# Gated recurrent cell: half B's h and z moved from fp32 to three bf16 parts, r of half B into half A's bank

## Chip, core and metric

The kernel runs on one core of one Trainium2 chip. The metric is the device time of one launch in microseconds, as the median of the runs. Times without a unit in this text are microseconds.

## What is computed

A gated recurrent layer over 512 time steps, with 8 sequences and 512 units, and the input added to its output:

```python
def step(h, x_t):
    fused = sigmoid(concat([x_t, h]) @ w_W + w_b)
    r, z = split(fused, 2)                      # "hidden_state", "output_state"
    m = x_t @ wx_W + wx_b + r * (h @ wh_W + wh_b)
    return z * h + (1.0 - z) * tanh(m)
out = x + scan(step, cond_1024, x)
```

All arrays are float32. x is (8, 512, 512), the weights are w_W (1024, 1024), wx_W (512, 512), wh_W (512, 512). Three products need the state of the step before: those of r, of z and of h (`h @ wh_W`); the products with x_t don't, and are made ahead of time.

## The kernel before

**Layout.** The 512 units lie as 4 chunks k of the contraction (128 partitions each) and, on the output side, as 4 column groups j of TensorE: a matmul with 32 columns of weights (the "weights" here are the state, 4 steps x 8 sequences, of which only the running step's 8 are not zero) writes PSUM partitions 32j to 32j+32. The moving operand is the model's weights. The output's 128 units of a group are split into half A (64) and half B (64), so that one half can be updated while the other is multiplied. Half A is chunks 0 and 1 of the state, half B chunks 2 and 3.

**TensorE.** Three PSUM tiles per group of 4 steps (two sets, used in turn) take the recurrent products: A holds h, z, r of half A (192 columns), B holds r and h of half B (128), C holds z of half B (64). The order within a step is written out by hand: `ORDER = "A0 B0 A1 A2 A3 B1 B2 B3 C0 C1 C2 C3"`, letter for tile, digit for chunk; each entry is 4 fp32 matmuls, one per column group. An fp32 matmul stands in the trace as two records. After them come 7 matmuls of the x products for a later group (`take(later, 7)`; 192 columns, into `xp`); they run out 11 steps before the end, and steps 0 to 4 take 8 or fewer of 384 columns in their place. The accumulated x side is copied into A, B, C ahead of a group by ScalarE (`spread`), and turned by VectorE (`turn_x`) for the part of m that r doesn't multiply.

**Everything else of a step**, in program order: `turn_r`, `turn_h`, `turn_z` of half A (VectorE transposes 32x32 blocks from PSUM: `tr`, `md1A`, `tz`; ScalarE takes sigmoids), `memory(0, q)` (a VectorE scan over pairs makes m, ScalarE's tanh follows, one for each chunk q), the transposes of r and h of half B, `update(0, 0)` (a scan over triples makes the new state of chunk 0), the transpose of z of half B, `update(0, 1)`, then `memory` and `update` of half B. The engines run their queues in order. `idle` memsets on VectorE carry waits. ScalarE copies the new state into the next step's scan input, GpSimd adds x for the output (`ot`, line 507), and SyncE stores chunks of 16 steps and loads x.

**Names and lines.** `mm` is line 188 for all matmuls; `act` line 216; `scan` line 358 (tiles `m`, `hTA`, `hTB`); `turned` line 374; `turn_h` line 390; `spread` line 251; `turn_x` line 256; idle memsets lines 400 and 505; output add line 507. `hT` is the state, `md0` and `md1` the scan inputs of `memory`, `hd0` that of `update`. The A0 of a step needs `update(0, 0)` of the step before, A1 needs `update(0, 1)`, A2 and A3 those of half B.

Of the kernel before, what the change touches and what calls it, by code (L numbers as in the profile page):

```python
# [21 lines left out]
DVE_FILL = 23  # L22
IDLE = 3
# [14 lines left out]
XP = {"A": slice(0, 192), "X": slice(192, 320), "C": slice(320, 384), "B": slice(384, 512)}  # L38
# [3 lines left out]
def tile_cond_rnn_residual(  # L42
# [5 lines left out]
    wa_d: bass.AP,  # L48
    wb_d: bass.AP,
    wb3_d: bass.AP,  # L50
# [76 lines left out]
    wa = const.tile([P, NQ, NQ, 192], F32, name="wa")  # L127
    for k in range(NQ):
        nc.sync.dma_start(out=wa[:, k], in_=wa_d[k])
    wb = const.tile([P, NQ, NQ, 192], F32, name="wb")  # L130
    nc.sync.dma_start(out=wb[:, :3], in_=wb_d)
    nc.sync.dma_start(out=wb[:, 3], in_=wb3_d)

    def wh(bank, k, j):
        return wa[:, k, j] if bank == "A" else wb[:, k, j, {"C": slice(0, 64), "B": slice(64, 192)}[bank]]
# [3 lines left out]
    def pair(n, name, rows, slots):  # L139

        return const.tile([P, 2, rows, slots], F32, name=name).rearrange("p c n s -> p n c s")

    NH = 2 * GS
    hT = [[pair(n, f"hT{n}{i}", 32, 3) for i in range(NH)] for n in "AB"]

    md0 = [[pair(n, f"md0{n}{i}", 32, 2) for i in range(2)] for n in "AB"]
    md1 = [[pair(n, f"md1{n}{i}", 32, 2) for i in range(2)] for n in "AB"]
    hd0 = [[pair(n, f"hd0{n}{i}", B, 3) for i in range(2)] for n in "AB"]  # L150
# [7 lines left out]
    for j in range(NQ):  # L158
        nc.vector.memset(ones[32 * j : 32 * j + 1, j], 1.0)

    nc.scalar.activation(const.tile([P, 1], F32, name="table"), zeros[:, :1], AF.Sigmoid)
    for n, t_ in enumerate(hd0[0] + hd0[1] + md0[0] + md0[1] + hT[0] + hT[1]):
# [3 lines left out]
    idle = const.tile([P, IDLE], F32, name="idle")  # L166
# [8 lines left out]
    def state(hf, i, slot=2):  # L175

        s = i % GS
        return hT[hf][i % NH][:, B * s : B * s + B, :, slot]

    ctx.enter_context(tc.manual_schedule())  # L180
    banks = [
        {n: psum.tile([P, w], F32, name=f"{n}{q}") for n, w in BANKS.items()}
        for q in range(2)
    ]
# [8 lines left out]
    for t_ in list(banks[0].values()) + list(banks[1].values()):  # L193
        mm(t_, none, none[:, :1].broadcast_to([P, t_.shape[1]]), start=True)
# [8 lines left out]
    nc.vector.tensor_copy(bias, xps[0])  # L203
    for hf in range(2):
        for slot in (0, 2):
            nc.vector.tensor_copy(
                state(hf, 0, slot), hin[:, 2 * hf : 2 * hf + 2].rearrange("p c b -> p b c")
            )
# [35 lines left out]
    def part(g, c0, c1):  # L244

        return late(g)[:, c0 - 256 : c1 - 256] if c0 >= 256 else xps[g % 2][:, c0:c1]

    def spread(g, names):

        for n in names:  # L250
            nc.scalar.copy(banks[g % 2][n], part(g, XP[n].start, XP[n].stop))

    def turn_x(g, e):

        c0 = XP["X"].start + 32 * e
        nc.vector.transpose(md1[e // 2][g % 2][:, :, e % 2, 1], part(g, c0, c0 + 32))
# [67 lines left out]
    spread(0, "BCA")  # L324
    for e in range(NQ):
        turn_x(0, e)

    pool_done = {}
    for i in range(T):
        g, s = divmod(i, GS)  # L330
        c, t = divmod(i, TC)
        ps = banks[g % 2]
# [5 lines left out]
        for n in (ORDER if i else FIRST).split():  # L338
            if n == "x":
                take(first[1], 1)  # L340
                continue
            bank, k = n[0], int(n[1])
            hs = hT[k // 2][i % NH][:, :, k % 2, 2]
            for j in range(NQ):
                j = (j + turn[0]) % NQ
                to = ps[bank] if i or bank != "A" else xps[0][:, XP["A"]]
                mm(to[32 * j : 32 * j + 32, :], hs, wh(bank, k, j))
# [8 lines left out]
        def scan(c_, out_, d0, d1):  # L356

            return nc.vector.tensor_tensor_scan(  # L358
                *[t_[:, :, c_].rearrange("p n c s -> p (n c s)") for t_ in (out_, d0, d1)],
                0.0,  # L360
                ALU.mult,
                ALU.add,
            ).ins

        pa = ps["A"] if i else xps[0][:, XP["A"]]
        raw = {
            "h": (pa[:, :HU], ps["B"][:, HU:]),
            "z": (pa[:, HU : 2 * HU], ps["C"]),
            "r": (pa[:, 2 * HU :], ps["B"][:, :HU]),
        }  # L370

        def turned(n, hf):
            t_ = work.tile([P, 2, 32], F32, tag=f"t{n}{hf}", name=f"t{n}{hf}_{i}")
            inst = nc.vector.transpose(t_.rearrange("p c n -> p (c n)"), raw[n][hf]).ins  # L374
            return t_[:, :, rows], inst

        r_done = [None, None]
        h_done = [None, None]

        def turn_r(hf):  # L380
            tr, _ = turned("r", hf)
            r_done[hf] = act(
                ("r", hf, g % 2, s),
                md0[hf][g % 2][:, rows, :, 1].rearrange("p n c -> p c n"),
                tr,
                AF.Sigmoid,
            )

        def turn_h(hf):
            inst = nc.vector.transpose(  # L390
                md1[hf][g % 2][:, :, :, 0].rearrange("p n c -> p c n"), raw["h"][hf]
            ).ins
            h_done[hf] = inst
            if hf == 0 and i + 1 - NH in pool_done:
                tc.add_manual_dep(inst, pool_done[i + 1 - NH].name, SYNC)

        def turn_z(hf):
            tz, _ = turned("z", hf)
            if hf == 0:
                inst = nc.vector.memset(idle[:, IDLE - 1 :], 0.0).ins  # L400
                tc.add_manual_dep(inst, h_done[0].name, SYNC)
            act(
                ("zc", hf, i % 2),
                hd0[hf][i % 2][:, :, :, 2].rearrange("p n c -> p c n"),
                tz,
                AF.Sigmoid,
                scale=-1.0,
            )

        ms = [  # L410
            work.tile([P, 2, B, 2], F32, tag=f"m{hf}", name=f"m{hf}_{i}").rearrange("p c n s -> p n c s")
            for hf in range(2)
        ]

        def memory(hf, q):

            c_ = slice(q, q + 1)
            scan(c_, ms[hf], md0[hf][g % 2][:, rows], md1[hf][g % 2][:, rows])
            act(("n", hf, q, i % NH), state(hf, i, 1)[:, :, c_], ms[hf][:, :, c_, 1], AF.Tanh)

        def update(hf, q):
            s1 = (i + 1) % GS
            new = hT[hf][(i + 1) % NH][:, B * s1 : B * s1 + B]
            return scan(slice(q, q + 1), new, hd0[hf][i % 2], hT[hf][i % NH][:, rows])

        turn_r(0)
        turn_h(0)
        turn_z(0)
        memory(0, 0)
        memory(0, 1)  # L430
        turn_r(1)
        turn_h(1)
        update(0, 0)
        turn_z(1)
        tc.add_manual_dep(update(0, 1), r_done[1].name, SYNC)
# [3 lines left out]
        if i == T - 1:  # L439
            nc.gpsimd.tensor_tensor(  # L440
                ot[:, t, :2, :].rearrange("p c n -> p n c"),
                x_of(c, slice(0, 2), t, 1).rearrange("p c n -> p n c"),
                state(0, T),
                ALU.add,
            )
        memory(1, 0)
        memory(1, 1)
        update(1, 0)
        update(1, 1)
        for hf in range(2):  # L450
            act(("h", hf, (i + 1) % NH), state(hf, i + 1, 0), state(hf, i + 1), AF.Copy)
# [3 lines left out]
        o, u = divmod(i, 2 * GS)  # L455
        nxt, two = o + 1 < NG // 2, o + 2 < NG // 2
        if i == 0:
            nc.scalar.copy(odd[0], xps[1][:, 256:512])
            spread(1, "A")
            turn_x(1, 0)  # L460
        ahead = 2 * o + (1 if u < 3 else 2 if u < 7 else 3)
        if ahead < NG:
            turn_x(ahead, (u + 1) % GS)
        if u == 0:
            spread(2 * o + 1, "B")
            if o and nxt:
                nc.scalar.copy(reg(GA), reg(BE))
        elif u == 1:
            spread(2 * o + 1, "C")
# [3 lines left out]
        elif u == 2 and nxt:  # L473
            last = odd[(o + 1) % 2][:, :HALF]
            nc.vector.tensor_tensor(last, reg(GA), both, ALU.add)
        elif u == 3 and nxt:
            if o:
                nc.vector.tensor_tensor(even[:, :HALF], reg(BE), both, ALU.add)
            spread(2 * o + 2, "A")
        elif u == 4 and nxt:  # L480
            if o == 0:
                nc.scalar.copy(odd[1], xps[1][:, 256:512])
            spread(2 * o + 2, "B")
# [3 lines left out]
        elif u == 5 and nxt:  # L487
            spread(2 * o + 2, "C")
# [6 lines left out]
        elif u == 7 and nxt:  # L495
            spread(2 * o + 3, "A")
# [7 lines left out]
        for n in range(IDLE - 1):  # L504
            nc.vector.memset(idle[:, n : n + 1], 0.0)
# [100 lines left out]
```

## Time and profile before

| | |
|---|---|
| median of 3 runs (lowest, highest) | 1679.92 (1678.17, 1680.07) |
| span of the profiled execution | 1670.8 |
| median less that span | 9.1 |
| mean granted TensorE clock | 0.999 |
| TensorE, VectorE, ScalarE, GpSimd busy | 1659.0, 1090.5, 1029.9, 301.9 |
| matmul records | 56238 |

The span runs from the first to the last instruction of one profiled execution; the runs' times hold what lies around it too. An engine's busy time is that in which one of its instructions ran; matmuls overlap in TensorE and their ends are modelled, so its share says that it always had a matmul under way, not that it worked at its full pace. In the timeline a row is the start, the duration, the engine, the line, the operation, output and inputs by the tiles' names, the shape, and how many like it follow (xN); in brackets stands the idle time before it and what ended it. In the rows of groups the total busy time and the mean ns of one stand behind the bar, then the engine's idle time before them.

### The profile page before, as it was taken

Reading aid. Unit: us, or ns where it says so; the run is one execution under the profiler, and the core shown is the slowest. Engines: PE = TensorE matmul, PEld = TensorE weight load, DVE = VectorE, ACT = ScalarE, POOL = GpSimd, SP = SyncE. Lnnn points to the kernel's source line nnn. Section 1 sums busy time; section 2 is a strip of 40 time slices with the busy share of each in tenths; the row PEclk is TensorE's granted clock in tenths of the full one; section 3 lists DMA queues with packets and bytes.
Section 4 is the critical chain, followed back from the end, with each engine's and each line's share of the span. In section 5 each row is a group of like instructions: output and inputs, shape, how many; then the busy total and the mean of one; then the engine's idle time right before and its main releaser. Section 6 shows DMA issues by size and latency. Waiting matters only on the chain.

```text
span 1670.8 us, 129875 instructions
## 1 busy us (share of the span) xinstructions
PE 1659.0 (99%) x56238; PEld 1637.5 (98%) x56238; DVE 1090.5 (65%) x9387; ACT 1029.9 (62%) x5822; POOL 301.9 (18%) x1281
## 2 busy tenths in 40 slices
PE   8999999999999999999999999999999999999998
PEld 5999999999999999999999999999999999999997
DVE  6666666666666666666666666666666666666666
ACT  3666666666666666666666666666666666666665
POOL 1111111111111111111111111111111111111111
PEclk9999999999999999999999999999999999999999
DMA  4000000000000000000000000000000000000000
GB/s 179 17 5 17 18 18 17 17 6 17 17 18 18 5 17 18 17 17 5 18 17 17 18 11 12 18 17 17 18 5 17 17 18 17 5 17 12 11 12 10
DMA packets 11525, 31.40 MB, mean 19 GB/s; under 512 B 1220, under 2 KB 1732, under 8 KB 10824
## 3 DMA queue, kind: packets, MB, share of 16 engines
q1 hardware_dynamic: 10800, 22.94, 4.0%
q8 instruction: 440, 7.21, 1.8%
q14 instruction: 133, 1.09, 0.2%
q10 hardware_dynamic: 152, 0.16, 0.0%
HBM read 14.70 MB, written 8.39 MB: 14 GB/s over the span
## 4 chain that ended last, share of the span: by engine, by line
PE 98%; DVE 1%; DMA 0%; issue 0%; ACT 0%
PE A L188 44%; PE B L188 23%; PE xp L188 20%; PE C L188 12%; DMA rows<-in_bias_dram 0%; DVE tr L374 0%; DVE m L358 0%; DVE tz L374 0%; DVE md1B L390 0%; DVE md1A L390 0%; DVE hTA L358 0%; DVE bias L203 0%; ACT hTB L216 0%; ACT xp L224 0%; DVE rows L120 0%
## 5 line engine op out<-in xcount | busy, mean ns | idle before, releaser
L188 PE MATMUL A<-wa,hTA 128*32 128x192 f32 x8176 | 638.2, 329 | 2.3 <-DVE hTA L358 2.3
L188 PE MATMUL B<-wb,hTA 128*32 128x128 f32 x8192 | 573.8, 273 | 0.0
L188 PE MATMUL A<-wa,hTB 128*32 128x192 f32 x8176 | 507.4, 326 | 0.5 <-DVE hTB L358 0.5
L188 PEld LDWEIGHTS B<-wb,hTA 128*32 128x32 f32 x8192 | 471.2, 122 | 1.4 <-issue 0.2
L374 DVE STREAM_TRANSPOSE tr<-A 128x64 f32<-128x64 f32 x511 | 127.7, 250 | 463.5 <-PE A L188 463.5
L188 PE MATMUL B<-wb,hTB 128*32 128x128 f32 x8192 | 398.9, 273 | 0.0
L188 PEld LDWEIGHTS A<-wa,hTA 128*32 128x32 f32 x8176 | 385.4, 123 | 7.6 <-DVE hTA L358 4.0
L188 PEld LDWEIGHTS A<-wa,hTB 128*32 128x32 f32 x8176 | 372.9, 122 | 2.7 <-DVE hTB L358 0.8
L216 ACT ACTIVATE md0A<-tr 128x16 f32<-128x16 f32 x512 | 112.3, 219 | 421.0 <-DVE tr L374 421.0
L507 POOL TENSOR_TENSOR ot<-xin,hTB 128x16 f32<-128x16 f32 x503 | 125.9, 250 | 1324.5 <-DVE hTB L358 1314.0
L188 PEld LDWEIGHTS B<-wb,hTB 128*32 128x32 f32 x8192 | 321.5, 122 | 0.1
L188 PE MATMUL C<-wb,hTA 128*32 128x64 f32 x8192 | 289.4, 219 | 0.0
L188 PE MATMUL C<-wb,hTB 128*32 128x64 f32 x8192 | 288.9, 220 | 0.2 <-issue 0.2
L188 PEld LDWEIGHTS C<-wb,hTA 128*32 128x32 f32 x8192 | 266.7, 122 | 0.0
L188 PE MATMUL xp<-tw,sx 128*32 128x192 f32 x2976 | 237.2, 326 | 0.1
L188 PEld LDWEIGHTS C<-wb,hTB 128*32 128x32 f32 x8192 | 229.2, 123 | 0.4 <-issue 0.4
L358 DVE TENSOR_TENSOR_SCAN hTB<-hd0B,hTB 128x24 f32<-128x24 f32 x1024 | 157.8, 195 | 101.0 <-ACT hTB L216 99.8
L358 DVE TENSOR_TENSOR_SCAN hTA<-hd0A,hTA 128x24 f32<-128x24 f32 x1024 | 191.0, 187 | 0.0
L188 PE MATMUL xp<-wx,xin 128*32 128x192 f32 (+1 forms) x2048 | 182.4, 331 | 0.7 <-issue 0.5
L216 ACT ACTIVATE hd0B<-tz 128x16 f32<-128x16 f32 x512 | 115.2, 225 | 93.7 <-DVE tz L374 93.7
L216 ACT ACTIVATE hTB<-hTB 128x16 f32<-128x16 f32 x512 | 120.5, 235 | 79.8 <-DVE hTB L358 72.3
L216 ACT ACTIVATE hTB<-m 128x8 f32<-128x8 f32 x1024 | 160.6, 206 | 0.0
(92 smaller groups left out, 2489.6 us busy)
## 6 DMA issues: line engine op xcount, KB each, us to landing
xin<-in_x_dram SPq DMA_DIRECT2D x31, 256.0 KB, 3.5
out_dram<-ot SPq DMA_DIRECT2D x31, 256.0 KB, 2.2
wx<-in_wx_dram SPq DMA_DIRECT2D x4, 768.0 KB, 7.1
wa<-in_wa_dram SPq DMA_DIRECT2D x4, 384.0 KB, 8.9
wb<-in_wb_dram SPq DMA_DIRECT2D x1, 1152.0 KB
wb<-in_wb_dram SPq DMA_DIRECT2D x1, 384.0 KB, 11.1
out_dram<-ot SPq DMA_DIRECT2D x1, 192.0 KB, 3.9
head<-in_xh_dram ACTq DMA_DIRECT2D x1, 144.0 KB, 5.0
```

Of the source, the lines that this page charges most:

```text
L188: nc.tensor.matmul(out_, lhsT, rhs, start=start, stop=False, skip_group_check=True)
L216: inst = nc.scalar.activation(out_, in_, func, **kw).ins
L358: return nc.vector.tensor_tensor_scan(*[t_[:, :, c_].rearrange("p n c s -> p (n c s)") for t_ in (out_, d0, d1)], 0.0, ALU.mult, ALU.add,).ins
L374: inst = nc.vector.transpose(t_.rearrange("p c n -> p (c n)"), raw[n][hf]).ins
L507: return engine.tensor_tensor(ot[:, t, 2 * hf : 2 * hf + 2, :].rearrange("p c n -> p n c"), x_of(c, slice(2 * hf, 2 * hf + 2), t, 1).rearr ...
```

## The change

- **One fp32 bank.** h, r, z of half A and r of half B share a bank `g` of 256 columns: entries A0, A1, A2 have 256 columns, chunk 3 is split into C3 (h and r of half A, 128 columns) and D3 (z of half A, r of half B).
- **bf16 parts.** h and z of half B are made last, in a bank `hz` of 128 columns. The state is split in three bf16 parts (the upper half of each fp32 word, of the rest, of the rest of that): `split`, two GpSimd subtractions a half and step, reading upper halves in place; ScalarE's copy (`copies_of`) writes the first part beside the copy that it made before. The three parts of 8 sequences are 24 columns of weights. The model's weights are split once, ahead of step 0, into three bf16 parts (`split_weights`, on ScalarE, VectorE and GpSimd). Each entry B0 to B3 is 3 x 4 bf16 matmuls. At step 0 they are fp32 instead.
- **Summing the parts.** `hz` has 3 x 8 rows for the parts and 8 rows that hold the bias of h. One 128x128 transpose brings it to `md1B`, where a scan over 5 elements (3 parts, bias, x side) makes m; for z a `tensor_reduce` sums the 5.
- **Order on VectorE.** Half A's two scans and two tanhs become one each; `beside()`, which holds `turn_x` (now 64 columns at a time) or a sum of 192 columns, stands between the transpose of z and the scan; the `idle` memsets go; `update(0, 0)` stands behind the transpose of `hz`. `update(0, 1)` stands behind the first scan of half B.
- GpSimd's output adds follow the splits, half A first. The x side goes to the bank in two copies of 128 columns.

```diff
-ORDER = "A0 B0 A1 A2 A3 B1 B2 B3 C0 C1 C2 C3"
-FIRST = "A0 x A1 x A2 x A3 B0 B1 B2 B3 C0 C1 C2 C3"
-BANKS = {"A": 192, "B": 128, "C": 64}
+ORDER = "A0 A1 A2 C3 D3 B0 B1 B2 B3"
+FIRST = "B0 B1 B2 B3 A0 x A1 x A2 x A3"
+COLS = {"A": slice(0, 256), "C": slice(0, 128), "D": slice(128, 256)}
...
+    def split(hf, i):
+        s = B * (i % GS)
+        nc.gpsimd.tensor_tensor(
+            part_of(hf, i, 1), state(hf, i), hi[hf][i % NH][:, :, s : s + B, 2], ALU.subtract
+        )
+        return nc.gpsimd.tensor_tensor(
+            part_of(hf, i, 2), part_of(hf, i, 1), part_of(hf, i, 1, hi), ALU.subtract
+        ).ins
...
+    banks = [psum.tile([P, 512], F32, name=f"g{q}")[:, :256] for q in range(2)]
+    hps = psum.tile([P, 512], F32, name="hz")[:, :128]
...
+            hs = hi[k // 2][i % NH][:, k % 2, 32 + B * s : 56 + B * s, 0]
+            for q in range(3):
+                for j in range(NQ):
+                    j = (j + turn[0]) % NQ
+                    mm(hps[32 * j : 32 * j + 24], hs, parts[:, k, q, j], start=(k == 0 and q == 0))
...
+        gate_r(0, turned(1))
+        nc.vector.transpose(
+            md1[0][g % 2][:, :, :, :, 0].rearrange("p s c b -> p c s b"), ps[:, :HU]
+        )
+        gate_z(0, turned(2))
+        beside()
+        memory(0, slice(0, 2))
+        gate_r(1, turned(3))
+        nc.vector.transpose(md1[1][g % 2][:, s].rearrange("p c b e -> p c e b")[:, :, :4], hps)
         update(0, 0)
-        turn_z(1)
-        tc.add_manual_dep(update(0, 1), r_done[1].name, SYNC)
+        zs = work.tile([P, 2, B], F32, tag="zs", name=f"zs_{i}")
+        nc.vector.tensor_reduce(zs, md1[1][g % 2][:, s, 2:], mybir.AxisListType.X, ALU.add)
+        gate_z(1, zs)
+        memory(1, slice(0, 1))
+        update(0, 1)
+        if i < T - 1:
+            act(("h", 0, (i + 1) % NH), *copies_of(0, i + 1), AF.Copy)
...
+        memory(1, slice(1, 2))
         update(1, 0)
         update(1, 1)
...
-        for n in range(IDLE - 1):
-            nc.vector.memset(idle[:, n : n + 1], 0.0)
...
+        split(0, i + 1)
+        add(0, nc.gpsimd)
+        split(1, i + 1)
+        pool_done[i + 1] = add(1, nc.gpsimd)
```

The weights' arrays are cut anew on the host side to match (`wh` for h and z of half B, `w4` for the bank of 256 columns); their bytes are the same.

More of the change, by code (lines that the diff above doesn't have):

```diff
@@ L125, in tile_cond_rnn_residual, with upper @@
         nc.sync.dma_start(out=wx[:, k], in_=wx_d[k])
-    wa = const.tile([P, NQ, NQ, 192], F32, name="wa")
+    whole = const.tile([P, NQ, NQ, 128], F32, name="whole")
     for k in range(NQ):
[L129 to L135, printed above, removed]
+        nc.sync.dma_start(out=whole[:, k], in_=wh_d[k])
+    w4 = const.tile([P, NQ, NQ, 256], F32, name="w4")
+    for k in range(NQ):
+        nc.sync.dma_start(out=w4[:, k], in_=w4_d[k])
+    parts = const.tile([P, NQ, 3, NQ, 128], BF16, name="parts")
+    rest = const.tile([P, NQ, NQ, 128], F32, name="rest")
     load_x(0, 1)
-    def pair(n, name, rows, slots):
-        return const.tile([P, 2, rows, slots], F32, name=name).rearrange("p c n s -> p n c s")
     NH = 2 * GS
[L146 to L150, printed above, removed]
+    hT = [[const.tile([P, 2, ROWS, 3], F32, name=f"hT{n}{i}") for i in range(NH)] for n in "AB"]
+    def upper(t_):
+        flat = t_.rearrange("p c r s -> p (c r s)").bitcast(BF16)
+        return flat.rearrange("p (c r s e) -> p c r s e", c=2, r=ROWS, s=3)[:, :, :, :, 1]
+    hi = [[upper(t_) for t_ in ts] for ts in hT]
+    md0 = [
+        [const.tile([P, GS, 2, B, ne], F32, name=f"md0{n}{i}") for i in range(2)] for n, ne in (("A", 2), ("B", NE))
+    ]
+    md1 = [
+        [const.tile([P, GS, nc_, B, ne], F32, name=f"md1{n}{i}") for i in range(2)]
+        for n, nc_, ne in (("A", 2, 2), ("B", 4, NE))
+    ]
+    hd0 = [[const.tile([P, 2, B, 3], F32, name=f"hd0{n}{i}") for i in range(2)] for n in "AB"]
     zeros = const.tile([P, 512], F32, name="zeros")
@@ L165, in tile_cond_rnn_residual @@
         nc.gpsimd.memset(t_[:, :, :, 1], -1.0)
-    idle = const.tile([P, IDLE], F32, name="idle")
+    for t_ in md0[1]:
+        nc.gpsimd.memset(t_, 1.0)
+        nc.gpsimd.memset(t_[:, :, :, :, 0], 0.0)
     tw = [const.tile([P, 2, NQ, HALF], F32, name=f"tw{n}") for n in range(4)]
@@ L203, in tile_cond_rnn_residual, with split_weights @@
     nc.vector.tensor_copy(bias, xps[0])
+    nc.vector.tensor_copy(whb_rows[:, :HU], rows4[:, 448:])
+    mm(hps, last8.rearrange("p j m -> p (j m)"), whb_rows, start=True)
     for hf in range(2):
[L205 to L208, printed above, removed]
+        nc.vector.tensor_copy(state(hf, 0), hin[:, 2 * hf : 2 * hf + 2])
+        nc.vector.tensor_copy(state(hf, 0, 0), hin[:, 2 * hf : 2 * hf + 2])
+    def split_weights():
+        for k in range(NQ):
+            nc.scalar.copy(parts[:, k, 0], whole[:, k])
+            e = nc.vector if k % 2 == 0 else nc.gpsimd
+            e.tensor_tensor(rest[:, k], whole[:, k], parts[:, k, 0], ALU.subtract)
+        for k in range(NQ):
+            nc.scalar.copy(parts[:, k, 1], rest[:, k])
+            e = nc.vector if k % 2 == 0 else nc.gpsimd
+            e.tensor_tensor(parts[:, k, 2], rest[:, k], parts[:, k, 1], ALU.subtract)
     turn = [0]
@@ L242, in late, with spread, turn_x @@
         return even if g % 2 == 0 else odd[g // 2 % 2]
[L244 to L256, printed above, removed]
+    def spread(g, n):
+        c = slice(128 * n, 128 * n + 128)
+        nc.scalar.copy(banks[g % 2][:, c], xps[g % 2][:, c])
+    def turn_x(g, n):
+        to, c = ((0, 0), (1, 0), (1, 2))[n]
+        nc.vector.transpose(
+            md1[to][g % 2][:, :, c : c + 2, :, NES[to] - 1].rearrange("p s c b -> p c s b"), late(g)[:, 64 * n : 64 * n + 64]
+        )
     def reg(r):
@@ L323, in tile_cond_rnn_residual @@
     weight_sum(2)
-    spread(0, "BCA")
-    for e in range(NQ):
-        turn_x(0, e)
+    spread(0, 0)
+    spread(0, 1)
+    for n in range(3):
+        turn_x(0, n)
+    split_weights()
     pool_done = {}
@@ L331, in tile_cond_rnn_residual @@
         c, t = divmod(i, TC)
-        ps = banks[g % 2]
+        ps = banks[g % 2] if i else xps[0][:, :256]
         if t == 0 and c > 0:
@@ L372, in turned @@
[L372 to L386, printed above, removed]
-            )
@@ L389, in turn_h @@
[L389 to L407, printed above, removed]
-            )
@@ L410, in tile_cond_rnn_residual @@
[L410 to L432, printed above, removed]
-        update(0, 0)
-        turn_z(1)
-        tc.add_manual_dep(update(0, 1), r_done[1].name, SYNC)
+        def scan(out_, d0, d1):
+            return nc.vector.tensor_tensor_scan(out_, d0, d1, 0.0, ALU.mult, ALU.add).ins
+        def turned(n):
+            t_ = work.tile([P, 2, 32], F32, tag=f"t{n}", name=f"t{n}_{i}")
+            inst = nc.vector.transpose(t_.rearrange("p c n -> p (c n)"), ps[:, 64 * n : 64 * n + 64]).ins
+            if n == 1 and i + 1 - NH in pool_done:
+                tc.add_manual_dep(inst, pool_done[i + 1 - NH].name, SYNC)
+            return t_[:, :, rows]
@@ new lines, in gate_r, with gate_z, memory @@
+        def gate_r(hf, tr):
+            act(("r", hf, g % 2, s), md0[hf][g % 2][:, s, :, :, NES[hf] - 1], tr, AF.Sigmoid)
+        def gate_z(hf, tz):
+            act(("zc", hf, i % 2), hd0[hf][i % 2][:, :, :, 2], tz, AF.Sigmoid, scale=-1.0)
+        def memory(hf, q):
+            ne = NES[hf]
+            m = work.tile([P, 2, B, ne], F32, tag=f"m{hf}{q}", name=f"m{hf}{q}_{i}")
+            scan(
+                *[
+                    t_.rearrange("p c b e -> p (c b e)")
+                    for t_ in (m[:, q], md0[hf][g % 2][:, s, q], md1[hf][g % 2][:, s, q])
+                ]
+            )
+            act(("n", hf, q, i % NH), state(hf, i, 1)[:, q], m[:, q, :, ne - 1], AF.Tanh)
@@ new lines, in update @@
+        def update(hf, q):
+            s1 = B * ((i + 1) % GS)
+            scan(
+                *[
+                    t_.rearrange("p b e -> p (b e)")
+                    for t_ in (
+                        hT[hf][(i + 1) % NH][:, q, s1 : s1 + B],
+                        hd0[hf][i % 2][:, q],
+                        hT[hf][i % NH][:, q, rows],
+                    )
+                ]
+            )
+        o, u = divmod(i, 2 * GS)
+        nxt, two = o + 1 < NG // 2, o + 2 < NG // 2
@@ new lines, in beside @@
+        def beside():
+            if u in (0, 1, 3) and i:
+                turn_x(2 * o + 1, min(u, 2))
+            elif u == 4 and o and nxt:
+                nc.vector.tensor_tensor(even[:, :HALF], reg(BE), both, ALU.add)
+            elif u > 4 and nxt:
+                turn_x(2 * o + 2, u - 5)
+        gate_r(0, turned(1))
+        nc.vector.transpose(
+            md1[0][g % 2][:, :, :, :, 0].rearrange("p s c b -> p c s b"), ps[:, :HU]
+        )
+        gate_z(0, turned(2))
+        beside()
```

110 lines of the change are left out of this document (46 added, 64 removed).

## The prediction

> **What bounds the kernel now.** I read the page first: its span, its busy shares and its chain.
>
> ```profile
> span 1670.8 us, 129875 instructions
> PE 1659.0 (99%) x56238; PEld 1637.5 (98%) x56238; DVE 1090.5 (65%) x9387; ACT 1029.9 (62%) x5822; POOL 301.9 (18%) x1281
> PE 98%; DVE 1%; DMA 0%; issue 0%; ACT 0%
> ```
>
> TensorE looks like the bound: busy 99% of the span, 98% of the chain. But these shares hide how close a second limit is, the loop through the state: the first matmul of a step (A0) needs half A's new state, which needs all of half A's matmuls of the step before. The last 11 of the 512 steps have no x products left to fill TensorE, and there the timeline shows that loop bare (start, duration, engine, operation; the weight loads and half B's rows are left out):
>
> ```profile
> 1660.94 0.55 PE L188 MATMUL A<-wa,hTA 128*32 128x192 f32 x8 [0.24 <-DVE hTA L358]
> ...
> 1661.31 0.40 PE L188 MATMUL B<-wb,hTA 128*32 128x128 f32 x8
> ...
> 1661.53 0.51 PE L188 MATMUL A<-wa,hTA 128*32 128x192 f32 x8
> ...
> 1661.85 0.83 PE L188 MATMUL A<-wa,hTB 128*32 128x192 f32 x16
> ...
> 1662.50 0.40 PE L188 MATMUL B<-wb,hTA 128*32 128x128 f32 x8
> ...
> 1662.75 0.25 DVE L374 STREAM_TRANSPOSE tr<-A 128x64 f32<-128x64 f32 x1 [0.94 <-PE A L188]
> 1662.93 0.21 DVE L390 STREAM_TRANSPOSE md1A<-A 128x64 f32<-128x64 f32 x1
> 1663.04 0.22 ACT L216 ACTIVATE md0A<-tr 128x16 f32<-128x16 f32 x1 [0.97 <-DVE tr L374]
> 1663.06 0.21 DVE L374 STREAM_TRANSPOSE tz<-A 128x64 f32<-128x64 f32 x1
> 1663.16 0.41 PE L188 MATMUL C<-wb,hTA 128*32 128x64 f32 x16
> 1663.22 0.06 DVE L400 MEMSET idle<- 128x1 f32 x1
> 1663.29 0.28 DVE L358 TENSOR_TENSOR_SCAN m<-md0A,md1A 128x16 f32<-128x16 f32 x2
> ...
> 1663.38 0.41 PE L188 MATMUL C<-wb,hTB 128*32 128x64 f32 x16
> 1663.48 0.23 DVE L374 STREAM_TRANSPOSE tr<-B 128x64 f32<-128x64 f32 x1
> 1663.51 0.31 ACT L216 ACTIVATE hTA<-m 128x8 f32<-128x8 f32 x2
> 1663.63 0.21 DVE L390 STREAM_TRANSPOSE md1B<-B 128x64 f32<-128x64 f32 x1
> ...
> 1663.77 0.20 DVE L358 TENSOR_TENSOR_SCAN hTA<-hd0A,hTA 128x24 f32<-128x24 f32 x1
> ...
> 1664.02 0.55 PE L188 MATMUL A<-wa,hTA 128*32 128x192 f32 x8 [0.24 <-DVE hTA L358]
> ```
>
> The loop is 1664.02 − 1660.94 = 3.08 us: 1.81 from A0 to the transpose of r (1660.94 to 1662.75) and 1.27 from there to the next A0 (sigmoid, scan, tanh, the update of hTA at 1663.77, 0.25 more to the matmul). The starts of the groups give the pace of the matmuls: 8 records of 192 columns take 0.32 (1661.53 to 1661.85), 8 of 128 columns 0.22, 16 of 64 columns 0.22. Eight records are one chunk of the state against one block of weights (4 column groups, 2 records to each fp32 matmul). Column for column the pace is one, 0.213 for 8 records of 128.
>
> Now a step with x products, and two rows for the mean step:
>
> ```profile
> 38.15 0.25 DVE L374 STREAM_TRANSPOSE tr<-A 128x64 f32<-128x64 f32 x1 [1.22 <-PE A L188]
> ...
> 1665.83 0.25 DVE L374 STREAM_TRANSPOSE tr<-A 128x64 f32<-128x64 f32 x1 [0.95 <-PE A L188]
> ```
>
> ```profile
> 1400.61 0.25 DVE L374 STREAM_TRANSPOSE tr<-A 128x64 f32<-128x64 f32 x1 [0.73 <-PE A L188]
> ...
> 1401.62 0.20 DVE L358 TENSOR_TENSOR_SCAN hTA<-hd0A,hTA 128x24 f32<-128x24 f32 x1
> ...
> 1401.88 0.36 PE L188 MATMUL A<-wa,hTA 128*32 128x192 f32 x1
> ...
> 1403.83 0.25 DVE L374 STREAM_TRANSPOSE tr<-A 128x64 f32<-128x64 f32 x1 [0.97 <-PE A L188]
> ```
>
> The rows at 38.15 and 1665.83 are steps 5 and 511: 506 steps in 1627.68 us, ten of them at 3.08, so a step with x products takes (1627.68 − 30.8)/496 = 3.22. There too A0 starts 1.27 after the transpose of r (1400.61 to 1401.88); only the way back is longer, 1.95 instead of 1.81, because x products still stream. So TensorE's own work is the bound by a narrow margin: the loop lies 0.14 us behind it.
>
> **The change part by part.** (1) *TensorE's work.* Before, by the pace above: 4 × 0.32 (A) + 4 × 0.213 (B) + 4 × 0.107 (C) = 2.56, and 7 x products (14 records of 192 columns) 0.56: 3.12 of the measured 3.22. After: A0, A1, A2 with 256 columns 3 × 0.427, C3 and D3 2 × 0.213, together 1.71; then 48 bf16 matmuls. No bf16 matmul stands in the loop of before; the nearest row is C, whose record also loads 32 columns of weights and streams as long as I estimate for 128 bf16 columns in one pass: 16 records in 0.22, 13.5 ns each, so 48 × 13.5 = 0.65. The bound above is an fp32 record of as many columns: 8 of 128 in 0.22, 27 ns each, 1.30. I take the C row, because columns times passes are the same. With x 0.56 that makes 2.92, 0.20 less than before, if TensorE still bound the step.
>
> A rule of the Trainium skill speaks against that price: "TensorE: Matmul & The Clock Gate", section "Wait — 56ns, not 53.3ns?", says that matmuls never start closer than about 25 ns however few columns they have. By it the 48 would take 1.20, close to the upper bound. The C rows (13.5 ns, over four column groups) do not agree with it; no bf16 row tests it here.
>
> (2) *The loop of half A, which decides.* Before, r, z and h of half A were complete after 4 × 0.32 + 0.213 (B0 in between) = 1.49 of matmuls. Now the bank also carries r of half B: 1.71. I looked for which matmul the first transpose waits: in the built program VectorE's wait for TensorE stands once, ahead of the transpose of r, and its count is that of the last matmul of D3, so splitting chunk 3 into C3 and D3 frees nothing early. A0 to the transpose of r becomes 1.81 + 0.21 = 2.02. The tail inside 1.81 (1.81 − 1.49 = 0.32) I keep; with a last matmul of 128 instead of 192 columns it could be 0.06 shorter (273 against 329 ns in the group rows).
>
> ```profile
> L188 PE MATMUL A<-wa,hTA 128*32 128x192 f32 x8176 | 638.2, 329 | 2.3 <-DVE hTA L358 2.3
> L188 PE MATMUL B<-wb,hTA 128*32 128x128 f32 x8192 | 573.8, 273 | 0.0
> ...
> L358 DVE TENSOR_TENSOR_SCAN hTA<-hd0A,hTA 128x24 f32<-128x24 f32 x1024 | 191.0, 187 | 0.0
> ...
> L216 ACT ACTIVATE hTA<-m 128x8 f32<-128x8 f32 x1024 | 160.4, 206 | 0.0
> ...
> L358 DVE TENSOR_TENSOR_SCAN m<-md0A,md1A 128x16 f32<-128x16 f32 x1024 | 142.1, 181 | 4.2
> ...
> L374 DVE STREAM_TRANSPOSE tr<-A 128x64 f32<-128x64 f32 x511 | 127.7, 250 | 463.5 <-PE A L188 463.5
> L507 POOL TENSOR_TENSOR ot<-xin,hTB 128x16 f32<-128x16 f32 x503 | 125.9, 250 | 1324.5 <-DVE hTB L358 1314.0
> ...
> L216 ACT ACTIVATE md0A<-tr 128x16 f32<-128x16 f32 x512 | 112.3, 219 | 421.0 <-DVE tr L374 421.0
> ```
>
> From there to A0 the same links stay, 1.27, with these changes. One scan and one tanh do both chunks, 32 and 16 elements: +0.02 (181 to 187 ns from 16 to 24 elements) and +0.01 (206 to 219). `beside()` now stands between the transpose of z and the scan; the idle memset goes. VectorE's starts are 0.18 and 0.13 apart for the transposes, so r, h, z and a fourth (0.15, as from r of half B to its h) put the scan at 0.18 + 0.13 + 0.13 + 0.15 = 0.59 against 0.54 today: +0.05 in 6 of 8 steps, none in one, about 0.17 in the one with the 192-column sum: +0.06 in the mean. Bounds: nothing, and a whole transpose, 0.25. The two separate wait instructions on VectorE I put at nothing (bounds 0 and the idle memset's 0.06 each). So 1.36.
>
> (3) *The update of hTA queued behind the transpose of hz.* That 128x128 transpose waits for the last bf16 matmul, and update(0,0) stands behind it. Counted from the end of D3's stream: B done at 0.65, visible 0.32 later, 0.97. The A chain brings VectorE there at 0.32 + 0.60 + 0.10 (scan) + 0.15 (transpose of r, B) = 1.17. So the wait is covered by 0.20; the transpose itself (0.13 to 0.25) lies beside the tanh, which ends the wait of update(0,0) at scan + 0.50.
>
> (4) *Half B.* After update(0,0) come the sum for z, a scan of 40 elements, update(0,1): starts of 0.10 to 0.13 each, so A1's state is there about 0.35 after A0's, and A1 starts 0.43 after A0. The sigmoid, the tanh and update(1,0) follow by about 0.8, A2 by 0.85. Both margins are under 0.1: price nothing, up to 0.1. GpSimd's parts are two more operations a half (0.25 each); after update(0,1) and 0.5 of splitting they are ready near 1.2 after update(0,0), and B0 starts near 2.0. Hidden; ScalarE's copies (0.22) likewise.
>
> (5) *Start.* The bytes of weights are the same. Splitting them puts eight copies and eight subtractions ahead of step 0; most of it waits for weights anyway: +1.5 (0 to 5). Steps 1 to 4, with 1.28 of x products each, gain about 0.2 each: −1. Together 0.
>
> **The sum.** A step is 2.02 + 1.36 = 3.38, with or without x products, which now fit into the loop's wait. 496 × (3.38 − 3.22) = 79, 11 × (3.38 − 3.08) = 3: +82 on 1670.8 gives a span of 1753. Around the span lie 1679.92 − 1670.8 = 9.1 to the median of the runs shown: **1762**. TensorE idles 3.38 − 2.92 = 0.46 a step: the saved work is real and buys nothing.
>
> **The rivals.** *A: r is not held by D3* (faster). If the transposes of r and h start when C3 is done, the loop loses D's 0.21: 3.17, TensorE's 2.92 still fits, and 496 × 0.05 less 11 × 0.09 is 24: **1656**. It decides from the point at which the first transpose starts under 1.86 after A0. For it: C3 covers r's columns. Against: the one wait, at D3's count. *B: bf16 at the pace of fp32.* At 27 ns the 48 take 1.30: hz is visible 1.62 after D3's stream, 0.45 past VectorE's 1.17; up to 0.1 of that is covered by the tanh: step 3.73 to 3.83, so about 3.78, 496 × 0.56 + 11 × 0.70 = 285: **1965**. It decides from 17.7 ns (0.65 + 0.20 over 48). For it: no row of such matmuls. Against: C's rows. By the Trainium skill's 25 ns ("TensorE: Matmul & The Clock Gate", same section) the same way gives about 1910, an estimate. *C: half B late.* Each margin of (4) overrun by 0.1 delays A1 or A2: 3.48, +132: **1812**.
>
> **How the numbers follow.** The forecast 1762 has 0.68, C 0.18, B 0.07, A and anything else that frees the loop 0.05, within 0.2% 0.02. What a measurement of this kernel can tell from no change is about 0.2%. The low end takes 2.02 + 1.27 with nothing added, 3.29: +37, 1717, and some of the 0.06 of the tail: 1710. The high end takes 0.15 above the forecast for the waits, `beside()` and C: 3.53, +159, 1839. So 1710 to 1840; faster 0.05, same 0.02, slower 0.93.
>
> **What would show it.** TensorE's busy share falls to about 90%, and its idle time stands before the first matmul on `g` with hTA, released by VectorE's hTA. The transpose of r starts about 2.02 after A0, and A0 1.36 after it, alike in steps with and without x products. bf16 records start about 13.5 ns apart. Wrong would be: A0 following the x products without a gap (A), the 128x128 transpose ending a long wait on TensorE (B), gaps before A1 or A2 (C).

## The result, and the profile after

The changed kernel takes 1799.17 (median of 4 runs, 1798.34 to 1800.02), the kernel before 1679.95: a ratio of 1.071 (95% interval 1.069 to 1.072). It is slower by 119; by the spans of the two profiled executions (1798.0 and 1670.8) by 127. The forecast was 1762, with 1710 to 1840 as its range. The page of the changed kernel, its span, busy shares and chain:

```profile
span 1798.0 us, 123440 instructions
...
PE 1696.5 (94%) x52116; PEld 1128.2 (63%) x52116; DVE 1219.5 (68%) x7221; ACT 991.8 (55%) x5188; POOL 711.9 (40%) x3332
...
PE 58%; DVE 36%; issue 4%; DVEq 1%; DMA 0%; ACT 0%; POOL 0%
```

The chain went from 98% on TensorE to 58%, and VectorE has 36% of it. So the time is no longer set by TensorE's queue but by a loop that leaves it. TensorE's busy share hardly shows that (94%), because the modelled ends of matmuls reach over gaps. The weight loads (PEld) show it: 98% before, 63% now. One step of the timeline (with x products, and with a 64-column transpose in `beside()`; GpSimd, most weight loads and most of half B are left out):

```profile
1661.54 0.25 DVE L415 STREAM_TRANSPOSE t<-g 128x64 f32<-128x64 f32 x1 [1.08 <-PE g L222]
1661.55 0.52 PE L222 MATMUL hz<-parts,hTB 128*24 128x128 bf16 x24
1661.71 0.21 DVE L464 STREAM_TRANSPOSE md1A<-g 128x64 f32<-128x64 f32 x1
1661.82 0.22 ACT L262 ACTIVATE md0A<-t 128x16 f32<-128x16 f32 x1 [0.57 <-DVE t L415]
1661.84 0.21 DVE L415 STREAM_TRANSPOSE t<-g 128x64 f32<-128x64 f32 x1
1661.89 0.51 PE L222 MATMUL xp<-wx,xin 128*32 128x192 f32 x8
1661.97 0.26 DVE L298 STREAM_TRANSPOSE md1B<-odd 128x64 f32<-128x64 f32 x1
...
1662.21 0.50 PE L222 MATMUL xp<-tw,sx 128*32 128x192 f32 x6
...
1662.33 0.22 ACT L262 ACTIVATE hTA<-ce(0, 2, None)_473_53715 128x16 f32<-128x16 f32 x1
1662.36 0.37 DVE L471 STREAM_TRANSPOSE md1B<-hz 128x128 f32<-128x128 f32 x1
...
1662.59 0.21 DVE L411 TENSOR_TENSOR_SCAN hTA<-hd0A,hTA 128x24 f32<-128x24 f32 x1
...
1662.85 1.11 PE L222 MATMUL g<-w,hTA 128*32 128x256 f32 x16
...
1663.07 0.18 DVE L411 TENSOR_TENSOR_SCAN hTA<-hd0A,hTA 128x24 f32<-128x24 f32 x1
...
1663.30 0.19 PEld L222 LDWEIGHTS g<-w,hTA 128*32 128x32 f32 x8 [0.27 <-DVE hTA L411]
...
1663.78 1.05 PE L222 MATMUL g<-w,hTB 128*32 128x256 f32 x24
...
1664.64 0.52 PE L222 MATMUL hz<-parts,hTA 128*24 128x128 bf16 x24
1664.97 0.25 DVE L415 STREAM_TRANSPOSE t<-g 128x64 f32<-128x64 f32 x1 [1.08 <-PE g L222]
```

Read it as the prediction read the loop of before. From the transpose of r (1661.54) to the next A0 (1662.85) are 1.31; before they were 1.27. From A0 to the transpose of r (1664.97) are 2.12; before they were 1.81 in the bare loop and 1.95 with x products. Together 3.43 against 3.22. The mean step is a little longer, because two of eight steps are. The transposes of r of steps 5 and 511 are

```profile
40.71 0.25 DVE L415 STREAM_TRANSPOSE t<-g 128x64 f32<-128x64 f32 x1 [0.80 <-PE g L222]
...
1792.94 0.25 DVE L415 STREAM_TRANSPOSE t<-g 128x64 f32<-128x64 f32 x1 [0.99 <-PE g L222]
```

so 506 steps take 1752.2, or 3.46 each, where the same steps took 1627.7 before. The bf16 matmuls run as priced: 24 from 1661.55, the x products behind them from 1661.89, 0.34 or 14 ns each. The last x products start at about 1662.4 (1662.21 + 0.50, less one duration of 0.33), and TensorE starts nothing more until A0 at 1662.85. Who waits for whom, as total, number and longest wait over the run, after and (last row) before:

```profile
DVE t L415 <- PE g L222: 528.0, 506, 1.1
ACT md0A L262 <- DVE t L415: 423.2, 511, 1.7
PEld g L222 <- DVE hTA L411: 419.1, 1018, 2.6
...
PEld g L222 <- DVE hTB L411: 118.0, 508, 0.5
```

```profile
PEld A L188 <- DVE hTA L358: 4.0, 11, 0.4
```

The weight loads of the bank `g` wait 419 for VectorE's update of hTA. Before, the weight loads waited 4.0 for it in all.

### The profile page after: what moved, and what is told of

It reads as the page before. It is cut to its first block, busy times and chain, and to the rows that moved or that the text cites. A ratio compares the mean times of both kernels' runs of the same rounds, so it can differ in the third digit from the quotient of the medians.

```text
span 1798.0 us, 123440 instructions
## 1 busy us (share of the span) xinstructions
PE 1696.5 (94%) x52116; PEld 1128.2 (63%) x52116; DVE 1219.5 (68%) x7221; ACT 991.8 (55%) x5188; POOL 711.9 (40%) x3332
## 4 chain that ended last, share of the span: by engine, by line
PE 58%; DVE 36%; issue 4%; DVEq 1%; DMA 0%; ACT 0%; POOL 0%
PE g L222 57%; DVE t L415 13%; DVE md1B L471 8%; DVE md1A L464 4%; DVE md1B L298 3%; DVE hTA L411 2%; DVE md1A L298 1%; DVE even L459 1%; PE xp L222 1%; DVEq L415 1%; PE hz L222 0%; DMA rows<-in_bias_dram 0%; DVE parts L253 0%; ACT parts L247 0%; DVE rest L249 0%
## 5 line engine op out<-in xcount | busy, mean ns | idle before, releaser
L415 DVE STREAM_TRANSPOSE t<-g 128x64 f32<-128x64 f32 x1533 | 349.8, 228 | 534.0 <-PE g L222 528.0
L222 PE MATMUL g<-w,hTA 128*32 128x256 f32 x8176 | 568.2, 395 | 93.4 <-DVE hTA L411 43.3
L222 PE MATMUL g<-w,hTB 128*32 128x256 f32 x12264 | 537.9, 308 | 0.0
L203 POOL TENSOR_TENSOR hTA<-hTA 128x16 f32<-128x16 f32 x511 | 112.7, 221 | 984.5 <-DVE hTA L411 12.1
L222 PEld LDWEIGHTS g<-w,hTB 128*32 128x32 f32 x12264 | 357.3, 122 | 193.7 <-DVE hTB L411 118.0
L222 PEld LDWEIGHTS g<-w,hTA 128*32 128x32 f32 x8176 | 193.7, 127 | 420.4 <-DVE hTA L411 419.1
L222 PE MATMUL hz<-parts,hTB 128*24 128x128 bf16 x12264 | 265.2, 219 | 0.0
L222 PE MATMUL hz<-parts,hTA 128*24 128x128 bf16 x12264 | 265.0, 219 | 0.0
L222 PEld LDWEIGHTS <-hTA 128*24 128x24 bf16 x12264 | 236.8, 111 | 0.0
L222 PEld LDWEIGHTS <-hTB 128*24 128x24 bf16 x12264 | 209.6, 111 | 0.1
L206 POOL TENSOR_TENSOR hTA<-hTA 128x16 f32<-128x16 f32 x511 | 130.0, 254 | 40.1
```

The costliest lines, as they stand in the source:

```text
L203: nc.gpsimd.tensor_tensor(part_of(hf, i, 1), state(hf, i), hi[hf][i % NH][:, :, s : s + B, 2], ALU.subtract)
L206: return nc.gpsimd.tensor_tensor(part_of(hf, i, 2), part_of(hf, i, 1), part_of(hf, i, 1, hi), ALU.subtract).ins
L222: nc.tensor.matmul(out_, lhsT, rhs, start=start, stop=False, skip_group_check=True)
```

## The experiments

Every experiment is the changed kernel with one edit or two, but for the last two, which edit the kernel before. Ratios are to the kernel before on the same chip. It took 1683.55 on the chip of the first four runs on record (no x products, wait on h, two banks, `beside()` late), 1677.00 on that of the next four and 1677.96 on that of the last two, so a difference of a few microseconds between two experiments can be the chips'; where it matters, the steps of the traces are given.

**Is TensorE's work the bound?** Leave x products out:

```diff
         else:
-            take(later, 7)
             turn[0] += 7
```

> Leaves out the x products of steps 5 to 500 (the x side of groups 4 and later is then wrong). Loop theory: they lie in TensorE's wait for the update of hTA, so the time stays within 5 us of 1799. Rival (TensorE's work bounds the step): 496 x 0.56 = 278 less, about 1520.

Measured 1796.2 (two runs). The waits of TensorE in that run:

```profile
PE g L222 <- DVE hTA L410: 411.2, 507, 1.2
```

0.56 of work a step went and 3 of 1799 came back (mean step 3.461 in place of 3.464); TensorE's hole in front of A0 is 411/507 = 0.81 instead. TensorE's work does not bound the changed kernel.

**The separate wait on VectorE.** The wait for GpSimd (`pool_done`) goes from the transpose of r to that of h, where the kernel before had it:

```diff
-            if n == 1 and i + 1 - NH in pool_done:
-                tc.add_manual_dep(inst, pool_done[i + 1 - NH].name, SYNC)
...
-        nc.vector.transpose(
+        inst = nc.vector.transpose(
             md1[0][g % 2][:, :, :, :, 0].rearrange("p s c b -> p c s b"), ps[:, :HU]
-        )
+        ).ins
+        if i + 1 - NH in pool_done:
+            tc.add_manual_dep(inst, pool_done[i + 1 - NH].name, SYNC)
```

> The wait for GpSimd moves from the transpose of r to that of h, as before the change, so that the transpose of r carries its wait for TensorE itself and no separate wait instruction stands ahead of it. Loop theory: the start of a step's first transpose comes 0.067 us earlier (the gap from the wait row to the transpose in the changed kernel), each step is as much shorter: 507 x 0.067 = 34, about 1765. Rival (the 0.07 is only the way in which the end of a 128-column matmul is seen): 1799.

Measured 1758.81 (1757.01 to 1760.99), ratio to before 1.044 (1.042 to 1.046). The page's first line and the ends of the way from A0 to the transpose of r in one step:

```profile
span 1759.2 us, 122936 instructions
```

```profile
1000.99 1.11 PE L222 MATMUL g<-w,hTA 128*32 128x256 f32 x16
...
1003.04 0.25 DVE L415 STREAM_TRANSPOSE t<-g 128x64 f32<-128x64 f32 x1 [1.01 <-PE g L222]
```

There are 504 instructions fewer (123440 − 122936), one a step. A0 to the transpose of r is 1003.04 − 1000.99 = 2.05 in place of 2.12. With two engines to wait for, the transpose of r has its wait for TensorE in an instruction of its own ahead of it. In the changed kernel's chain this is the row DVEq, in the step shown above:

```profile
1664.90 0.02 DVEq L415
...
1664.97 0.25 DVE t L415
```

The transpose starts 0.067 after that row; with one engine to wait for, it carries the wait itself. 507 × 0.067 = 34 of the 40 gained (by the traces, the mean step is 3.384 in place of 3.464). The rest goes with one long step of every eight, which is gone too; the next run looks at it.

**`beside()` to the end of the step.**

```diff
         gate_z(0, turned(2))
-        beside()
         memory(0, slice(0, 2))
...
         update(1, 0)
         update(1, 1)
+        beside()
```

> beside() goes from between the transpose of z and the scan to the end of the step. The steps without any beside() are no shorter than those with a 64-column transpose, only the step with the 192-column sum (+0.124) and the first of a group pair (+0.147) are longer. If both go: 63 x 0.27 = 17 less, 1782; if only the sum goes: 8 less, 1791. The theory on record (0.06 us a step) would give 30 less, 1769.

Measured 1783.39 (1782.92 to 1786.19), 16 less than the change (mean step 3.433): both longer steps are gone, but for 0.02 of u = 0. Here u is the step's number within its eight. In the changed kernel, three of its steps on VectorE, u = 0, 2 and 4 (only the first transpose, what stands beside, and the update):

```profile
383.32 0.25 DVE L415 STREAM_TRANSPOSE t<-g 128x64 f32<-128x64 f32 x1 [1.08 <-PE g L222]
383.50 0.21 DVE L464 STREAM_TRANSPOSE md1A<-g 128x64 f32<-128x64 f32 x1
383.74 0.25 DVE L415 STREAM_TRANSPOSE t<-g 128x64 f32<-128x64 f32 x1
...
384.52 0.21 DVE L411 TENSOR_TENSOR_SCAN hTA<-hd0A,hTA 128x24 f32<-128x24 f32 x1
```

```profile
390.33 0.25 DVE L415 STREAM_TRANSPOSE t<-g 128x64 f32<-128x64 f32 x1 [1.08 <-PE g L222]
...
391.38 0.21 DVE L411 TENSOR_TENSOR_SCAN hTA<-hd0A,hTA 128x24 f32<-128x24 f32 x1
```

```profile
397.19 0.25 DVE L415 STREAM_TRANSPOSE t<-g 128x64 f32<-128x64 f32 x1 [1.08 <-PE g L222]
...
397.62 0.32 DVE L459 TENSOR_TENSOR even<-xp,both 128x192 f32<-128x192 f32 x1
...
398.36 0.21 DVE L411 TENSOR_TENSOR_SCAN hTA<-hd0A,hTA 128x24 f32<-128x24 f32 x1
```

From the first transpose to the update: 1.20, 1.05, 1.17. The step with nothing beside (u = 2) is no shorter than the one with a transpose shown further up (1661.54 to 1662.59, 1.05): there the sigmoid of r ends just as late as VectorE's extra transpose. The 192-column sum costs 0.12. In u = 0 the transpose of z starts 0.24 behind that of h instead of 0.13. Why, no run settled. With the wait on h the delay is gone. With `beside()` late it is still there, as a step u = 0 of this run shows, but it hardly costs any more, as nothing stands between z and the scan:

```profile
656.61 0.21 DVE L464 STREAM_TRANSPOSE md1A<-g 128x64 f32<-128x64 f32 x1
656.86 0.25 DVE L415 STREAM_TRANSPOSE t<-g 128x64 f32<-128x64 f32 x1
```

**Both edits.**

> The wait on h and beside() at the end of the step, both. If both lie on the loop of half A they add: 1799 - 40 - 16 = 1743. Rival (half B, whose margin was small, takes over): 1755 to 1760, no better than the wait alone.

Measured 1753.98 (1753.19 to 1755.31), ratio 1.046 (1.045 to 1.048). Neither number: the long step u = 0 had been counted in both edits (with the wait on h alone, it is already gone). 63 × 0.12 = 8 are left for `beside()`, and 1758.8 − 8 = 1751 is near what was measured. In the traces of the two versions A0 to the transpose of r is the same 2.05, and from there to A0 the mean falls from 1.332 to 1.319, so half B did not take over. By the intervals of their ratios to the kernel before, which of the two versions is faster isn't told.

**The update of hTA behind hz.**

```diff
-        nc.vector.transpose(md1[1][g % 2][:, s].rearrange("p c b e -> p c e b")[:, :, :4], hps)
         update(0, 0)
+        nc.vector.transpose(md1[1][g % 2][:, s].rearrange("p c b e -> p c e b")[:, :, :4], hps)
```

> update(0, 0) stands ahead of the transpose of hz instead of behind it. Theory (the queue behind hz costs nothing, since the tanh of half A ends just as late): update(0, 0) gains nothing, the transpose of hz moves behind the wait for the tanh, from 0.22 us before update(0, 0) to 0.09 behind it, and half B is that much later; A2 has nearly no room left: step + 0.25 to 0.3, 1920 to 1960. Rival (the update was late because of hz): 1799 or less.

Measured 1991.44 (two runs), slower still than expected. VectorE's queue and TensorE's, in one step:

```profile
1005.30 0.21 DVE L411 TENSOR_TENSOR_SCAN hTA<-hd0A,hTA 128x24 f32<-128x24 f32 x1 [0.15 <-ACT hTA L262]
1005.43 0.40 DVE L472 STREAM_TRANSPOSE md1B<-hz 128x128 f32<-128x128 f32 x1
...
1006.16 0.18 DVE L411 TENSOR_TENSOR_SCAN hTA<-hd0A,hTA 128x24 f32<-128x24 f32 x1
```

```profile
1005.56 0.65 PE L222 MATMUL g<-w,hTA 128*32 128x256 f32 x8 [0.30 <-DVE hTA L411]
1006.40 0.65 PE L222 MATMUL g<-w,hTA 128*32 128x256 f32 x8 [0.18 <-DVE hTA L411]
```

The update now waits 0.15 for the tanh, where before the edit the transpose of hz ran: the queue behind hz did cost nothing (from the transpose of r to the update are 1.05 with either order). But the transpose of hz now stands between update(0, 0) and update(0, 1), and A1 follows A0 by 0.84, where its columns need 0.43 and a start of 0.05 (A1 is what became late, not A2 as expected).

**Can r be freed by C3?** One bank as two PSUM tiles:

```diff
-ORDER = "A0 A1 A2 C3 D3 B0 B1 B2 B3"
+ORDER = "C0 D0 C1 D1 C2 D2 C3 D3 B0 B1 B2 B3"
...
-    banks = [psum.tile([P, 512], F32, name=f"g{q}")[:, :256] for q in range(2)]
+    banks = [[psum.tile([P, 512], F32, name=f"{n}{q}")[:, :128] for n in "cd"] for q in range(2)]
```

> The bank of 256 columns becomes two PSUM tiles of 128, so that the transposes of r and h wait for C3 alone; order C0 D0 C1 D1 C2 D2 C3 D3, then B as before. Loop theory: r starts 0.213 earlier, the transpose of hz has just room for it, step 3.46 - 0.21 = 3.25, 507 x 0.213 = 108: about 1691. Rival (TensorE's work or half B bounds): 1780 to 1800. Rival (the wait for hz then ends last): part of the gain, 1700 to 1750.

Measured 1951.26 (1948.43 to 1961.05), ratio 1.160 (1.157 to 1.164): all three expectations fell. The loop did what it should: in a step of that run,

```profile
1001.18 0.44 PE L222 MATMUL c<-w,hTA 128*32 128x128 f32 x8
...
1003.12 0.25 DVE L418 STREAM_TRANSPOSE t<-c 128x64 f32<-128x64 f32 x1 [0.87 <-PE c L222]
```

A0 to the transpose of r is 1.94, 0.18 less. That is one of the quicker steps; the median is 2.02. For TensorE lost time elsewhere that no wait in the profile accounts for: its waits named "issue" grew from none to four rows.

```profile
PE hz L222 <- issue: 57.5, 135, 1.8
PE d L222 <- issue: 25.1, 65, 1.1
PE c L222 <- issue: 23.1, 55, 1.4
PE xp L222 <- issue: 17.6, 43, 0.9
```

The edit had brought 12 more fp32 matmuls a step. An fp32 matmul is two weight loads and two matmul records, so 48 more instructions, 252 a step for 204. A new theory came of it: TensorE gets its instructions no faster than about 14.9 ns each. It was put to the test by the order alone, in one bank:

```diff
-ORDER = "A0 A1 A2 C3 D3 B0 B1 B2 B3"
+ORDER = "C0 D0 C1 D1 C2 D2 C3 D3 B0 B1 B2 B3"
```

> One bank as in the change, but A0, A1, A2 are made in two halves of 128 columns, order C0 D0 C1 D1 C2 D2 C3 D3 B0 B1 B2 B3: the same columns, banks and waits, 12 more fp32 matmuls a step (48 more instructions of TensorE: 252 for 204). New theory for the run with two banks (TensorE gets its instructions no faster than about 14.9 ns each, 3.74 us for 252): about 1940. Rival (instructions cost nothing, the two banks' waits did it): 1799.

Measured 1927.77 (1923.39, 1932.15): 129 more than the change, with the same columns, bank and waits. And from the other side, two banks without x products:

> Two banks again, and the x products of steps 5 to 500 left out (their x side is then wrong): 224 instructions of TensorE a step. Theory (instructions): 224 x 14.9 ns = 3.34 us, a little over the loop's 3.25, so 1690 to 1735. Rival (something else of the two banks makes the step 3.74): 1930 to 1950, as leaving out the x products cost nothing to the change.

Measured 1741.07 (two runs), just above the range: 210 less than with them, where the change gained 3 without them. In its trace the median step takes 3.26, which is the loop that the two banks were to give (A0 to the transpose of r 1.92), the mean 3.35. So with x products the instructions are the limit of the two-bank version; the last section shows what holds them. To let the single bank's transpose of r go ahead of D3 without a second bank was not tried: VectorE would read a PSUM bank while TensorE writes it.

**And the kernel before?** Its 220 instructions in 3.22 are 14.6 ns each, so it might sit at the same limit. The kernel before, with x products in two halves, for two of seven and then for all (the edit of the second is shown):

```diff
-                    mm(reg(to)[32 * j : 32 * j + 32], lhs[:, k], rhs[:, k, j])
+                    to_, rhs_ = reg(to)[32 * j : 32 * j + 32], rhs[:, k, j]
+                    for c0 in (0, 96):
+                        mm(to_[:, c0 : c0 + 96], lhs[:, k], rhs_[:, c0 : c0 + 96])
                     yield
```

> The kernel before, with two of the seven x products of a step made in two halves of 96 columns: the same columns, 228 instructions of TensorE a step for 220. If the kernel before is bound by the columns that TensorE streams (the prediction's 3.12 of 3.22): unchanged, 1677 to 1684. If it is bound by its instructions (220 in 3.22 us are 14.6 ns each): 8 x 0.0146 = 0.117 a step, 496 x 0.117 = 58 more, about 1738.

> The kernel before, with all seven x products of a step in two halves of 96 columns: 248 instructions a step. Columns: unchanged, 1677 to 1690. Instructions: 28 x 0.0146 = 0.41 a step, 203 more, about 1883.

Measured 1719.57 (1715.46 to 1730.08; ratio 1.025, 1.020 to 1.030) and 1864.40 (ratio 1.111, 1.108 to 1.114). The first lies between its two numbers, the second near that of the instructions: 42 more for 8 instructions a step and 186 more for 28, so 10.5 and 13.4 ns for each (over 496 steps). The second run's waits again carry "issue":

```profile
PE C L188 <- issue: 24.1, 66, 0.8
PE B L188 <- issue: 11.8, 36, 0.9
...
```

The columns were the same, and two halves take little longer than one whole: without the gaps over 0.1, the records of `xp` start 22 ns apart in this run and 40 ns apart before. So the time is in the gaps. The kernel before stands at the edge: its columns take 3.12, its loop 3.08, and 220 instructions at the 14.5 to 14.9 ns of the runs with 248 and 252 would take 3.19 to 3.28. Which of its columns and its instructions sets its 3.22 is not shown; its own trace has hardly any such gaps (last section).

## Why the prediction was right, step by step

- **What bounds the kernel now: half right.** That the loop lies close behind TensorE held, and decided the case. That the bound in front of it is the columns that TensorE streams is not shown: eight more instructions at equal columns already cost 42, so its instructions are as near. It did not matter to the sum, since the change lowers them to 204 (about 3.0 at 14.7 ns), under the loop.
- **TensorE's work (1): right.** bf16 at 14 ns each, as the C rows had it. The 25 ns of the Trainium skill's rule ("TensorE: Matmul & The Clock Gate", section "Wait — 56ns, not 53.3ns?") did not show, over four column groups. The saving buys nothing (no x products: 1796).
- **The loop of half A (2): right mechanism, one size off.** D's 0.21 was there, and the transpose of r waited for D3 (with two banks it came 0.18 earlier). Forecast 2.02 from A0 to the transpose of r, measured 2.12. The step that failed is "the two separate wait instructions on VectorE I put at nothing (bounds 0 and the idle memset's 0.06 each)": the one ahead of the transpose of r costs 0.067, 34 in all, shown by the wait on h. The other 0.03 is in A1: A0 to A2 takes 0.93 (1662.85 to 1663.78), where A0's and A1's columns are 0.85 and a start 0.05. A1's weight loads wait 0.27 for `update(0, 1)` (1663.07) and start at 1663.30, and A1's second half starts 0.24 behind its first, where that of A2 starts 0.22 behind. No run moved this wait alone.
- **From r to A0: right.** 1.36 forecast in the mean; 1.31 in most steps, 0.12 to 0.15 more in two of eight. `beside()` was priced at 0.06 in the mean, as 0.05 in six steps and 0.17 in one; it costs nothing in those six, 0.12 in the one with the sum, and the step u = 0 was not foreseen. So 1.36 was near in part by luck: of the 0.06 most was put on steps that cost nothing, and half of the 0.03 that came in the mean is u = 0.
- **The update behind hz (3): right**, the tanh ends as late; putting the update first cost 192.
- **Half B (4): right that it was near, about 0.03 a step out of "nothing, up to 0.1", in A1.** The state for A1 was expected 0.08 ahead of it, and its loads had to wait. A2's wait too (0.23, 1663.73), but A2 follows A1's last records at the usual pace. GpSimd's parts were late in no step of the trace: B0 starts 0.09 behind D3's last record in all of them.
- **The sum.** Forecast +82 on the span, measured +127: 124.5 in 506 steps and 2.6 ahead of them (the transpose of r of step 5 at 40.71 instead of 38.15; term 5 had put nothing there). Of the 45 missing, 34 are the wait instruction, about 15 (0.03 × 507) A1 and 2.6 the start; from r to A0 it was 8 less than forecast (1.344 in the mean, not 1.36). The rest is within the rounding of these terms. Of the 9.1 that the prediction laid around the span there were 1.2 in the changed kernel (1799.17 − 1798.0), and 2.3 to 2.6 in the executions of the kernel before that ran beside the experiments: the profiled one was some 7 shorter than usual. So the medians show an error of 37 and these two spans one of 45.
- **Rivals.** A (r freed by C3) fell: it needs a second bank, and then instructions bound. B (bf16 at fp32's pace) fell. C (a margin of (4) overrun by 0.1) came in part, 0.03 in A1.
- **What would show it.** The gap before A0 was there, and the steps with and without x products are alike. TensorE's busy share "about 90%" was 94%: the share of the weight loads is the better sign.

No version of the change tried beats the kernel before; of those that make the x products, the one with the wait on h is the nearest, 4.2 to 4.6% slower, and the one with both edits (4.5 to 4.8%) is not told from it.

## What to carry to other kernels

Where a kernel goes round a recurrence, price a change on two sums: the engine's work in a step, and the loop from one result through the other engines back to it; work that is saved outside the loop is worth nothing once the loop is longer, and columns that are added ahead of the loop's first reader are paid in full. Columns moved into a PSUM bank delay every reader of that bank, where the program's wait is set on the whole bank as here. Count instructions as well as columns: many small matmuls can cost more than the columns they stream.

## What the runs showed of the hardware

- **TensorE's instructions come in blocks of 256, and here a block every 3.7 at the most.** Steps of 252 and of 248 instructions took about 14.5 to 15 ns for each, with "issue" gaps, though bursts run faster (48 bf16 matmuls and their loads, 96 instructions, at 7 ns each). In the runs with two banks and with the order alone the page's row of the instruction queue (packets, MB, share) is

```profile
q8 instruction: 507, 8.31, 1.8%
```

  so 16 KB a packet. The following counts are from the traces between 50 and 1640. TensorE makes 256 records (matmuls and weight loads) for each packet. In the run with two banks, 358 gaps of over 0.2 between the starts of its records end at a record that waits for no semaphore, 202 in all. Every one of them ends 1.15 to 1.65 after a packet of this queue has landed, and no two after the same packet, though such moments are only 13% of the time. In the run with all x products split there are 294, all alike, and they hold 135 of the 186 that it lost; in the kernel before six, 2.5 in all. So TensorE stood waiting for its next block; decoding would not tie its gaps to packets. (No run changed the fetch itself.) The packets start 3.80 apart in the mean with two banks, 3.76 with the order alone, 3.72 in both runs with split x products, 3.74 in the kernel before and 4.30 in the change: 3.72 for 256 is 14.5 ns an instruction. The Trainium skill ("Runtime: NRT & Kernel Launch", section "Instruction fetch mechanics") says that instructions are fetched in blocks of 256 and that this is hidden behind their issue. The packets agree with the blocks; that TensorE's supply is hidden does not fit these runs.
- **A wait in an instruction of its own is not free on a loop:** 0.067 on VectorE between the wait and the transpose that follows it.
- **A wait that covers a whole PSUM bank costs its first readers the rest of the bank.** The reader of columns 0 to 127 had to wait for the writer of columns 128 to 255, because the program's wait counts to the last matmul of the bank; with a second bank the transpose of r came 0.18 earlier in the step shown. The Trainium skill ("PSUM — Partial Sum Buffer", section "PSUM bank collisions raise a hardware error") says to guard PSUM by bank and quadrant, not by address; no run here reads a bank while it is written.
